# A graph-network kernel in groups: two entries in the first and last group, four between, and first products from features that TensorE turns

## The chip, the cores and the metric

The kernel runs on one core of a Trainium2 chip. The metric is the device time of one execution in microseconds (us), as the median of several runs. The engines are TensorE (PE: matrix products and transposes), VectorE (DVE), ScalarE (ACT), GpSimd (POOL, which here issues the indirect DMAs) and SyncE (SP, which issues plain DMAs). Each engine works through its own instructions in order.

## The reference

There are 32 batch entries of 512 nodes with 256 features, and one 512x512 matrix `adj` in which few cells are not zero. Four layers follow each other: a graph layer with a gate for each edge, two plain layers, and a second graph layer with other weights.

```python
def gnn(h, A, W1, b1, W2, b2, Wa, ba, Wm, bm, beta1, beta2, beta3):   # layers 0 and 3
    pre_u = einsum('bud,dk->buk', h, W1[:d])
    pre_v = einsum('bvd,dk->bvk', h, W1[d:])
    hidden = relu(pre_u[:, :, None, :] + pre_v[:, None, :, :] + b1)
    S = sigmoid(einsum('buvk,ko->buvo', hidden, W2)[..., 0] + b2[0])
    a_t = einsum('buv,bud->bvd', S * A, h)
    m_t = einsum('uv,bud->bvd', A, h) * h
    return beta1*h + beta2*(a_t @ Wa + ba) + beta3*(m_t @ Wm + bm)

def layer1(z):                                    # z + relu(A z W^T + b)
    return z + relu(einsum('bid,ed->bie', einsum('ij,bjd->bid', A, z), W) + b)

def layer2(x):
    feats = einsum('bni,oi->bno', x, W1)
    f1 = einsum('bno,o->bn', feats, W2) + b2[0]
    coefs = softmax(leaky_relu(f1[:, :, None] + f1[:, None, :]) + A, axis=-1)
    return einsum('bij,bjo->bio', coefs, feats) + bias2 + x
```

S is needed only where `adj` is not zero. The kernel computes it there alone.

## The kernel before, in words

**Groups.** The entries are worked on in eight groups of four (`NB = 4`). A group goes through five stages, each a Python generator whose pieces are woven into one program.

- `first` (line 806): for each entry, load the features h, turn them on TensorE (`turned`, line 571), and form the products with W1 (`pre`, line 582: lines 592 and 594 on TensorE, 596 to 600 on DVE and ACT). The products go to a table in DRAM, one row for each node and side, with the group's four entries beside each other (4 x 256 values, 4 KB). The turned features are written to DRAM as `xT` (line 819).
- `edges` (line 650) of layer 0, here called an edge round: 36 items of 128 edges. For an item POOL fetches 128 table rows with an indirect DMA (`fetch`, line 644), DVE adds the row of the other node (line 731) and takes relu times W2, and the sum over features comes either from DVE itself, one entry at a time (line 747), or from ACT (line 717) after one DVE instruction for all entries (line 739). After the sigmoid (lines 614, 618, 619) and the factor from `adj` (line 675), POOL puts 128 cells of four values into a DRAM array with another indirect DMA (`put`, line 637). The rows of the other node ("mine") come by plain loads from SP (line 692) or, for four items, by an indirect DMA.
- `middle` (line 839): loads the group's cells as dense matrices (`load`, line 766, 1 MB each, four of them), and then does for each entry the rest of layer 0, layers 1 and 2, and the first products of layer 3 (`middle_one`, line 876). ACT first copies one entry's matrix out of the four (`flat`, line 857); line 891 is its first product.
- `edges` of layer 3, with its own table and cells.
- `last` (line 1094): the rest of layer 3 for each entry: the products hWa and mhT, then the sums with S (line 1061) and with Wm (line 1073).

**The two ends.** For the first group the products hWa and mhT are made ahead of its middle (`middle_before`, line 824), from h (line 867) and from the turned features loaded back from `xT` (line 871, in `fresh`). Its middle then takes them as `given`. For the last group `last` is split: `last_before` (line 1016) makes all that doesn't need S, `last_behind` (line 1039) the sums with S. In the edge rounds of these two ends ACT does all of the sums and more buffers hold fetched rows (`spare`).

**The cells.** One pair of cell arrays for each layer is zeroed once (`zeros`, line 555, eight plain DMAs issued by POOL; layer 0 in the opening, layer 3 in `zeros_behind`, line 550, after a DVE memset), and each group writes the same cells again. A put waits for the zeros and for the loads of the group before.

**The order.** `weave` (line 454) sorts the pieces of all stages by due times that are written out by hand in `sparse_path` (line 1162): one group's middle is one unit long, the middle of group 0 starts at 0. `edge_times` and `spread` (lines 1130 to 1143) spread the pieces of a stage evenly. `first` and `last` fill in where a middle leaves room on TensorE. Due times set an order and nothing else; what is late then holds up what stands behind it on its engine.

```python
        start, end = (max(0.0, k - 0.47) for k in (t, t + 1))
        ...
        edges3 = edge_times(end + 0.003, end + 0.05, end + 0.48, end + 0.54)
        behind = end + 0.56, end + 1.16
```

Of the kernel before, what the change touches and what calls it, by code (L numbers as in the profile page):

```python
# [38 lines left out]
GROUP = NB * D  # L39
# [364 lines left out]
class Group:  # L404
# [3 lines left out]
    def __init__(self, sp, w, name):  # L408
        self.w = w
        self.table = sp.dram.tile([2 * N, GROUP], F32, name=f"table_{name}")  # L410
        self.cells = sp.cells[name[0]]
        self.layer = name[0]
        self.puts = [f"puts_{name}_{q}" for q in range(2)]
        self.written = [[], []]
        self.s = sp.grp.tile([P, ITEMS, NB], F32, name=f"s{name[0]}")
        self.self_s = sp.grp.tile([P, NC, NB], F32, name=f"self_s{name[0]}")
# [6 lines left out]
class Sparse:  # L423
# [3 lines left out]
    def __init__(self, ctx, m, counts, xr, outr, B):  # L427
# [7 lines left out]
            k: [self.dram.tile([CELLS + SPARE, NB], F32, name=f"cells_{k}{q}") for q in range(2)] for k in "03"  # L435
# [11 lines left out]
        self.later, self.bigs, self.given, self.marks = None, 0, None, {}  # L447
        self.main = None
        self.before = {(k, q): [] for k in "03" for q in range(2)}
# [80 lines left out]
    def setup(self):  # L530
# [4 lines left out]
        self.zero = self.act.tile([P, GROUP], F32, name="zero", tag="hWa3")  # L535
# [8 lines left out]
        self.zeros("0")  # L544
# [5 lines left out]
    def zeros_behind(self):  # L550
        self.behind(self.nc.vector.memset(self.zero, 0.0))
        self.zeros("3")
        yield

    def zeros(self, layer):
        for h, c in enumerate(self.cells[layer]):
            flat = c[0:CELLS, :].rearrange("(q p a) b -> q p (a b)", q=4, p=P)
            for q in range(4):
                ins = self.nc.gpsimd.dma_start(flat[q], self.zero)
                self.before[layer, h].append(ins.ins.name)  # L560
# [21 lines left out]
    def pre(self, g, b, hT):  # L582

        nc, w = self.nc, g.w
        rows = g.table.rearrange("(c p k) (b d) -> p c k b d", p=P, k=2, b=NB)
# [41 lines left out]
    def written(self, g, half, ins):  # L627

        ins = ins.ins
        self.tc.declare_no_dep(ins, group=g.puts[half], reason="no two of a group's puts share a cell")
        self.tc.add_to_no_dep_group(g.puts[half], ins)
        self.after(ins, self.before[g.layer, half], "cells zeroed, and read by the group before")
        g.written[half].append(ins.name)
# [14 lines left out]
    def edges(self, g, spare=(), own_tags=()):  # L650
# [12 lines left out]
        def own_1():  # L663
            self.sigmoid_of(own)
            diag = self.counts.diag.unsqueeze(2).to_broadcast([P, NC, NB])
# [6 lines left out]
        def run_1(ks):  # L672
            self.sigmoid_of(g.s[:, ks, :].rearrange(flat))
            value = e.value[:, ks].unsqueeze(2).to_broadcast([P, ks.stop - ks.start, NB])
# [7 lines left out]
        def fetch(n):  # L682
            if n == EARLY:
                for j, tag in zip(panels, own_tags):
                    mine[-j] = self.act.tile([P, GROUP], F32, name="mine_more", tag=tag)
# [3 lines left out]
            if c not in mine:  # L689
                t = self.gath.tile([P, GROUP], F32, name="mine", bufs=3)  # L690
# [7 lines left out]
            if tag := tags[n % len(tags)]:  # L698
                rows = self.act.tile([P, GROUP], F32, name="rows_more", tag=tag)
            else:  # L700
                rows = self.gath.tile([P, GROUP], F32, name="rows")
# [11 lines left out]
        def sums(k, rows):  # L713

            for b in range(NB):
# [11 lines left out]
        for k in range(ITEMS):  # L727
# [8 lines left out]
            if spare or k % 2 == 1 and k < ITEMS - 3:  # L736
                by_entry = rows.rearrange("p (b d) -> p b d", b=NB)
                w2 = w["W2bc"].unsqueeze(1).to_broadcast([P, NB, D])
# [4 lines left out]
            else:  # L743
                for b in range(NB):
# [21 lines left out]
    def load(self, g, layer):  # L766

        tiles, loads = [], [[], []]
        for c in range(NC):
            t = self.act.tile([P, N, NB], F32, name=f"SA{layer}", bufs=NC)  # L770
# [7 lines left out]
        for q, names in enumerate(loads):  # L778
            self.before[g.layer, q] = names
# [26 lines left out]
    def first(self, g, i):  # L806
# [8 lines left out]
        for b in range(NB):  # L815
            ahead = load(b + 1) if b < NB - 1 else None
# [7 lines left out]
    def middle_before(self, g0, i):  # L824

        self.given = []
        for b in range(NB):
            h, hT = self.fresh(i + b)
            hT = hT()
# [7 lines left out]
            self.given.append((hWa, mhT))  # L837

    def middle(self, g0, g3, i):
# [3 lines left out]
        given, self.given = self.given, None  # L843
        h, hT = self.fresh(i, given)
        hT = hT()
        hWa = None
        if not given:
# [3 lines left out]
        for b in range(NB):  # L851
# [24 lines left out]
    def middle_one(self, g0, g3, b, i, SA, keep, given):  # L876
# [3 lines left out]
        if given:  # L880
            hWa, mhT = given[b]
# [19 lines left out]
        more = b < NB - 1  # L901
        if more:
            keep[0], turned = self.fresh(i + 1, given)
# [24 lines left out]
        if more:  # L928
            keep[1] = turned()
            ahead = None if given else self.hWa(g0, keep[1], 0)  # L930
# [85 lines left out]
    def last_before(self, g, i):  # L1016

        self.ends = []
        for b in range(NB):
# [19 lines left out]
    def last_behind(self, g, i):  # L1039
        SA = self.load(g, 3)  # L1040
        for b in range(NB):
# [52 lines left out]
    def last(self, g, i):  # L1094
# [6 lines left out]
        for b in range(NB):  # L1101
            for hWa in self.hWa(g, hT, 3):
                yield
            if done is not None:
                nc.sync.dma_start(self.outr[i + b - 1], done)
                if b < NB - 1:
# [3 lines left out]
            if b < NB - 1:  # L1110
# [3 lines left out]
        nc.sync.dma_start(self.outr[i + NB - 1], done)  # L1114
# [11 lines left out]
FIRST, LAST, AHEAD = even(NB * 5 + 1), even(NB * 8 + 1), even(NB * 4 + 1)  # L1126
ENDS, BEHIND = even(NB * 6 + 1), even(NB * 2 + 1)
# [18 lines left out]
def middle_shares(given):  # L1146


    hWa = [] if given else [1.7, 1.7]
    shares = list(hWa)  # L1150
    for b in range(NB):
        more = hWa if b < NB - 1 else []
        shares += [] if given else [2.8, 2.8]
# [8 lines left out]
def sparse_path(ctx, m, counts, xr, outr, B):  # L1162
# [3 lines left out]
    last = B // NB - 1  # L1166
# [4 lines left out]
        (sp.zeros_behind(), spread(even(2), 0.15, 0.2), ""),  # L1171
    ]
    for t in range(last + 1):
        g0, g3 = Group(sp, m.g0, f"0_{t}"), Group(sp, m.g3, f"3_{t}")
        start, end = (max(0.0, k - 0.47) for k in (t, t + 1))

        if t == 0:
            first = spread(FIRST, -0.385, -0.30)
            edges0 = edge_times(-0.292, -0.27, -0.03, -0.02, LEAD_AT_ENDS)
        elif t == 1:  # L1180
            first = spread(FIRST, -0.28, -0.06)
# [268 lines left out]
```

## Time and profile before

| what | value |
|---|---|
| runs of the kernel before | 2991.82, 2996.85, 2997.82 us; median 2996.85 us |
| profiled execution | 2998.45 us, with a span of 2996.8 us |
| PE busy | 2690.0 us (90%) |
| DVE busy | 2307.1 us (77%) |
| POOL busy | 1555.3 us (52%) |
| ACT busy | 1336.8 us (45%) |
| moved by DMA | 677.30 MB, mean 226 GB/s |
| POOL fetches of rows (line 646) | 552 of 1230 ns |
| POOL puts of cells (line 639) | 576 of 1211 ns |

The span is what the profiler sees of one execution; the profiled execution's own time lies 1.65 us above it. A line such as L731 is line 731 of the kernel before. "Busy" counts an engine's own instructions, not its waits; a share is one of the whole span and hides that stages differ. The page also cuts the span into 40 equal slices and gives each engine's busy tenths in each. "PEclk" is the clock that TensorE was granted, in tenths of full speed. A row in a table of windows gives the window, its length, and the busy time (with the number of instructions) of PE, of PE's weight loads, of DVE, ACT and POOL, then the granted clock, the share of the DMA engines and the bytes moved. In a timeline, the bracket at the end of a row gives the idle time before it and what ended that.

### The profile page before, as it was taken

The numbers are of one execution on the slowest core, as the hardware profiler recorded it, in microseconds if no ns is written. First come the engines' busy times: TensorE is split into PE (matmuls) and PEld (weight loads), VectorE is DVE, ScalarE is ACT, GpSimd is POOL, SyncE is SP. The second block draws the span as 40 slices with busy tenths as digits, with TensorE's granted clock in tenths as the row PEclk, the third lists the DMA queues.
The fourth block names the chain that finished last, engine by engine and source line by source line (L and its number), as shares of the span: only waits on it lengthen the run. The fifth ranks groups of instructions, "written<-read, shape, count | busy, mean of one in ns | idle before, by whom it ended". The sixth has DMA issues, their size and how long they took to land. (4 is left out here: it accounts for less than half of the span.)

```text
span 2996.8 us, 32453 instructions
## 1 busy us (share of the span) xinstructions
PE 2690.0 (90%) x8645; PEld 1613.9 (54%) x8646; DVE 2307.1 (77%) x6035; ACT 1336.8 (45%) x4101; POOL 1555.3 (52%) x1328
## 2 busy tenths in 40 slices
PE   6367787989998999989999899989999899988998
PEld 3134344545664566546664466646565466644666
DVE  6874786889588885988778885888858896783494
ACT  3553454445344443544344443445434453453262
POOL 2662463646445673556536464466735564361183
PEclk9678998999999999999999999999999999999999
DMA  8875657796678867787677866687677866663474
GB/s 268 286 225 169 213 174 221 233 300 203 217 217 269 268 211 227 230 262 254 209 222 247 275 207 230 216 268 253 211 228 236 303 227 197 208 211 102 148 244 150
DMA packets 302143, 677.30 MB, mean 226 GB/s; under 512 B 52608, under 2 KB 170880, under 8 KB 293760
## 3 DMA queue, kind: packets, MB, share of 16 engines
q0 software_dynamic: 122688, 414.40, 42.9%
q1 hardware_dynamic: 160304, 223.52, 23.0%
q10 hardware_dynamic: 18960, 37.24, 3.4%
q8 instruction: 70, 1.15, 0.2%
q14 instruction: 121, 0.99, 0.1%
HBM read 529.02 MB, written 146.01 MB: 225 GB/s over the span
## 5 line engine op out<-in xcount | busy, mean ns | idle before, releaser
L646 POOL DMA_INDIRECT rows<-table,iv x552 | 679.0, 1230 | 795.5 <-DMA table<-puv 262.7
L639 POOL DMA_INDIRECT cells<-s,cell x576 | 697.6, 1211 | 420.6 <-DVE s L675 243.2
L731 DVE TENSOR_TENSOR rows<-rows,mine 128x1024 f32<-128x1024 f32 x552 | 666.4, 1215 | 101.4 <-DMA rows<-table,iv 72.8
L717 ACT ACTIVATE rows<-rows 128x256 f32<-128x256 f32 x1088 | 439.6, 406 | 445.4 <-DVE rows L739 396.6
L46 PE MATMUL pst<-adj,h 128*128 128x512 f32 x1024 | 452.2, 592 | 0.0
L747 DVE SCALAR_TENSOR_TENSOR rows<-rows,L_gnn_W2bc 128x256 f32<-128x256 f32 x1120 | 414.0, 417 | 1.6
L739 DVE SCALAR_TENSOR_TENSOR rows<-rows,L_gnn_W2bc 128x1024 f32<-128x1024 f32 x272 | 329.4, 1213 | 0.4
L46 PEld LDWEIGHTS pst<-adj,h 128*128 128x128 f32 x1024 | 192.8, 190 | 219.9 <-issue 217.6
L46 PE MATMUL pst<-L_gnn_Wa,hT 128*128 128x256 f32 x1024 | 248.8, 393 | 62.9 <-DMA hT<-xT 57.8
L46 PEld LDWEIGHTS pst<-L_gnn_Wa,hT 128*128 128x128 f32 x1024 | 198.9, 199 | 103.0 <-issue 59.2
L46 PE MATMUL pst<-eT,feats 128*128 128x512 f32 x512 | 237.7, 619 | 10.9 <-ACT eT L1004 10.9
L46 PE MATMUL pst<-adjT,zW 128*128 128x512 f32 x512 | 228.2, 599 | 11.6 <-ACT zW L916 9.7
L596 DVE TENSOR_TENSOR puv<-pst,bc_L_gnn_b 128x256 f32<-128x256 f32 x256 | 104.9, 416 | 162.4 <-DMA table<-puv 89.2
L597 ACT COPY puv<-pst 128x256 f32<-128x256 f32 x256 | 93.2, 371 | 288.1 <-DVE puv L596 225.9
L1061 PE MATMUL pst<-hWa,SA 128*128 128x256 f32 x896 | 220.3, 400 | 0.0
L1061 PEld LDWEIGHTS pst<-hWa,SA 128*128 128x128 f32 x896 | 213.8, 328 | 3.7 <-issue 1.7
L717 ACT ACTIVATION_READ_ACCUMULATOR rows<-rows 128x1 f32 x1088 | 204.7, 188 | 0.0
L860 ACT COPY flat<-SA 128x512 f32<-128x512 f32 x128 | 136.7, 1128 | 136.6 <-issue 62.9
L891 PE MATMUL pst<-flat,hWa 128*128 128x512 f32 x448 | 196.8, 592 | 0.0
L592 PE MATMUL pst<-w_L_gnn_W,hT 128*128 128x512 f32 x256 | 141.5, 681 | 53.9 <-ACT hT L579 36.5
L46 PEld LDWEIGHTS pst<-eT,feats 128*128 128x128 f32 x512 | 99.9, 198 | 133.2 <-issue 113.3
L46 PEld LDWEIGHTS pst<-adjT,zW 128*128 128x128 f32 x512 | 96.5, 191 | 133.4 <-issue 114.0
(176 smaller groups left out, 3984.2 us busy)
## 6 DMA issues: line engine op xcount, KB each, us to landing
table<-puv SPq DMA_DIRECT2D x256, 256.0 KB
SA<-cells POOLq DMA_DIRECT2D x64, 1024.0 KB
h<-in_x_dram SPq DMA_DIRECT2D x64, 512.0 KB
mine<-table SPq DMA_DIRECT2D x64, 512.0 KB
hT<-xT SPq DMA_DIRECT2D x36, 512.0 KB
xT<-hT ACTq DMA_DIRECT2D x32, 512.0 KB
x2T<-yT SPq DMA_DIRECT2D x32, 512.0 KB
x2s<-x ACTq DMA_DIRECT2D x64, 256.0 KB
```

Of the source, the lines that this page charges most:

```text
L46: nc.tensor.matmul(out, lhsT, rhs, start=(n == 0), stop=(n == len(pairs) - 1))
L592: nc.tensor.matmul(pp, hT[:, 0, ks], w["W1"][:, 0::DC, :], start=True, stop=False)
L596: nc.vector.tensor_tensor(puv[:, 0, :], pp[:, 0:D], w["b1bc"], ALU.add)
L639: ins = self.nc.gpsimd.indirect_dma_start(out=g.cells[half], out_offset=bass.IndirectOffsetOnAxis(ap=at, axis=0), in_=s, in_offset=None)
L646: self.nc.gpsimd.indirect_dma_start(out=rows, out_offset=None, in_=g.table, in_offset=bass.IndirectOffsetOnAxis(ap=at, axis=0))
L717: self.behind(nc.scalar.activation(part, part, AF.Identity, accum_out=g.s[:, k, b : b + 1]))
L731: self.behind(nc.vector.tensor_tensor(rows, rows, other, ALU.add))
L739: nc.vector.scalar_tensor_tensor(by_entry, by_entry, 0.0, w2, ALU.max, ALU.mult)
L747: nc.vector.scalar_tensor_tensor(part, part, 0.0, w["W2bc"], ALU.max, ALU.mult, accum_out=at)
L860: self.nc.scalar.copy(flat[:, r, :], SA[r][:, :, b])
L891: nc.tensor.matmul(pz, hWa[:, r, cs], flat[:, r, :], start=(r == 0), stop=False)
L1061: self.nc.tensor.matmul(pz[:, k * D : (k + 1) * D], SA[r][:, cs, b], hWa[:, r, :], start=(r + k == 0), stop=(alone and k == 1 and r == NC ...
```

## The change

The 32 entries go in nine groups of 2, 4, 4, 4, 4, 4, 4, 4 and 2. A group carries its size `n`, and tables, cells, row buffers and loops go by it. There are cell arrays for both sizes, each zeroed: those for layer 0 with two entries in the opening, those with four entries a little later, and layer 3's two sizes in the first middles. `middle_before` still makes four entries' hWa and mhT: the two of group 0 and the first two of group 1. It turns their features on TensorE with `turned` in place of loading `xT`; the middle still loads `xT` for its own use. The due times are written anew. Cut to its core:

```diff
-GROUP = NB * D
+FEW = 2
 class Group:
-    def __init__(self, sp, w, name):
+    def __init__(self, sp, w, name, n):
-        self.table = sp.dram.tile([2 * N, GROUP], F32, name=f"table_{name}")
+        self.table = sp.dram.tile([2 * N, n * D], F32, name=f"table_{name}")
-        self.cells = sp.cells[name[0]]
+        self.cells = sp.cells[name[0], n]
 ...
-    def zeros_behind(self):
-        self.behind(self.nc.vector.memset(self.zero, 0.0))
-        self.zeros("3")
-        yield
+    def zeros_behind(self, of):
+        for k in of:
+            self.behind(self.nc.vector.memset(self.zero, 0.0))
+            self.zeros(*k)
+            yield
 ...
     def middle_before(self, g0, i):
-        self.given = []
         for b in range(NB):
-            h, hT = self.fresh(i + b)
-            hT = hT()
+            h, _ = self.fresh(i + b)
+            hT = self.turned(h, "hT1")
 ...
-            self.given.append((hWa, mhT))
+            self.given[i + b] = hWa, mhT
 ...
+LENGTHS = {0: 0.4, 1: 0.87}
+GIVEN = {0: FEW, 1: NB - FEW}
 ...
-    last = B // NB - 1
+    sizes = [FEW] + [NB] * ((B - 2 * FEW) // NB) + [FEW]
+    last = len(sizes) - 1
 ...
-        (sp.zeros_behind(), spread(even(2), 0.15, 0.2), ""),
+        (sp.zeros_behind([("0", NB)]), spread(even(2), -0.2, -0.15), ""),
+        (sp.zeros_behind([("3", FEW), ("3", NB)]), spread(even(3), 0.15, 0.45), ""),
 ...
-    for t in range(last + 1):
-        start, end = (max(0.0, k - 0.47) for k in (t, t + 1))
+    at, end = 0, 0.0
+    for t, n in enumerate(sizes):
+        start, end = end, end + (0.4 if t == last else LENGTHS.get(t, 1.0))
         if t == 0:
-            first = spread(FIRST, -0.385, -0.30)
+            first = -0.385, -0.345
             edges0 = edge_times(-0.292, -0.27, -0.03, -0.02, LEAD_AT_ENDS)
+            edges3 = edge_times(end + 0.003, end + 0.02, end + 0.3, end + 0.33)
+            behind = end + 0.4, end + 0.8
         elif t == 1:
-            edges0 = edge_times(0.02, 0.07, start - 0.06, start - 0.04)
+            edges0 = edge_times(0.01, 0.03, start - 0.05, start - 0.03)
 ...
         if t == last - 1:
-            edges3 = edge_times(end + 0.003, end + 0.05, end + 0.46, end + 0.5)
-            behind = end + 0.7, end + 1.06
+            edges3 = edge_times(end + 0.003, end + 0.04, end + 0.38, end + 0.4)
+            behind = end + 0.44, end + 0.6
         if t == last:
-            end -= 0.2
-            edges3 = edge_times(end + 0.003, end + 0.02, end + 0.45, end + 0.46, LEAD_AT_ENDS)
-            behind = end + 0.29, end + 0.45
+            edges3 = edge_times(end + 0.003, end + 0.02, end + 0.3, end + 0.31, LEAD_AT_ENDS)
+            behind = end + 0.21, end + 0.3
 ...
-            streams.append((sp.last_behind(g3, t * NB), spread(BEHIND, end + 0.5, end + 0.6), ""))
+            times = spread(even(BEHIND * n + 1), end + 0.35, end + 0.42)
+            streams.append((sp.last_behind(g3, at), times, ""))
```

In `middle_one`, an entry's hWa and mhT are looked up by its number (`if i in given`), so that a middle may have some entries' products given and make the others'.

## The prediction

> **What bounds the kernel now.** I read the busy shares by slice first. TensorE (PE) is at nine tenths nearly everywhere except in the first ten or so slices, and there its granted clock falls too.
>
> ```profile
> PE   6367787989998999989999899989999899988998
> DVE  6874786889588885988778885888858896783494
> PEclk9678998999999999999999999999999999999999
> ```
>
> Then I cut the span where the first matmul of line 891 of each group's middle stands, and where the last of line 594 ends, and asked for busy times by window (columns: window, length, busy us of PE, weight loads, DVE, ACT, POOL, granted clock, DMA share, GB/s). I call the stretches opening, main 0, main 1, a steady main (mains 2 to 6 last 344.6, 346.1, 349.4, 343.6 and 343.6), main 7 and tail.
>
> ```profile
> 0.00:245.20 245.20, 135.81 (x389) 74.36 (x391) 174.92 (x437) 114.28 (x426) 127.88 (x125) 0.80 0.79 260
> 245.20:485.20 240.00, 195.90 (x561) 103.66 (x560) 159.06 (x423) 113.08 (x291) 94.74 (x87) 0.89 0.56 183
> 485.20:824.20 339.00, 308.86 (x985) 181.41 (x984) 277.24 (x757) 154.20 (x462) 193.00 (x162) 0.97 0.74 237
> 1168.80:1514.90 346.10, 328.44 (x1073) 197.35 (x1072) 281.93 (x764) 155.01 (x464) 188.71 (x161) 0.99 0.73 238
> 2551.50:2817.60 266.10, 246.51 (x779) 145.37 (x778) 165.22 (x432) 107.73 (x285) 87.89 (x79) 0.97 0.47 149
> 2817.60:2996.80 179.20, 160.16 (x576) 121.87 (x574) 121.03 (x166) 72.60 (x317) 99.96 (x80) 0.96 0.66 218
> ```
>
> The reader is to see that a steady main is PE-bound (328 of 346 us), while opening and main 0 hold 109 and 44 us of idle PE. The tail holds only 19. So an earlier first main is what there is to win, and the price is paid where a main becomes short against the edge round beside it.
>
> Third, the opening and the round that follows it, and entries of main 7 (its last has no round items beside it):
>
> ```profile
> 82.00:235.00 153.00, 70.49 (x185) 38.93 (x184) 121.73 (x244) 79.86 (x341) 101.97 (x80) 0.71 0.76 253
> 240.00:451.00 211.00, 170.33 (x485) 89.38 (x483) 147.51 (x388) 100.56 (x267) 93.61 (x85) 0.90 0.57 184
> ...
> 2551.50:2626.80 75.30, 74.57 (x253) 46.87 (x252) 59.16 (x148) 33.94 (x99) 30.32 (x27) 1.00 0.66 213
> 2626.80:2695.60 68.80, 57.96 (x165) 31.71 (x164) 59.50 (x150) 36.00 (x113) 47.34 (x41) 0.90 0.65 203
> 2757.60:2817.60 60.00, 60.00 (x199) 37.06 (x198) 18.15 (x42) 14.76 (x30) 0.00 (x0) 1.00 0.08 27
> ```
>
> The first two edge rounds run from 82 to 235 and from 240 to 451. The same cut for the adds of line 731 alone (one to an item) says that main 7's first two entries have 16 and 18 items beside them:
>
> ```profile
> 2551.50:2626.80 75.30, 18.67 (x16) 1.00 0.66 213
> 2626.80:2695.60 68.80, 21.25 (x18) 0.90 0.65 203
> ```
>
> Last, waits in the opening and the end of the chain:
>
> ```profile
> PE pst L46 <- DMA hT<-xT: 57.8, 4, 25.7
> ```
>
> ```profile
> 220.70 1.24 POOL L639 DMA_INDIRECT cells<-s,cell  x1 [7.47 <-ACT big L791]
> ```
>
> ```profile
> 2958.43 5.13 DMA SA<-cells
> 2963.60 27.92 PE pst L1061 x118
> ```
>
> **The change, part by part.** The order of both programs gives the counts. PE gains 32 instructions (4 entries x 8 transposes); POOL gains 168: two rounds of 76 (36 fetches, 4 panel or "mine" fetches, 36 puts), 8 cell loads, 8 zero writes. SP goes from 592 to 600: four hT loads go, two rounds bring 8 "mine" loads and 4 diagonal writes. No entry's work goes. PE work of an entry, by the chain's rows: middle 6.87 (L891) + 3.43 (L898) + 3.45 (L912) + 6.9 (yT) + 3.5 (L934) + 2.2 (turns) + 6.9 (feats) + 6.87 (first products) + 0.88 = 41.0; hWa and mhT 10.3; its `first` 0.87 + 6.87 = 7.7; its `last` 3.45 + 6.87 + 7.7 (L1061) + 3.45 = 21.5.
>
> *Opening, 245 to 198.* The first fetch starts at 81.9, when four entries are in the table. Entry two's table writes are issued at 52.4 for 3.5 us, and the first index list is ready at 57.2 (DVE, L394): with two entries the first fetch is at 57. Round 0 on DVE now takes 36 x (1.2 + 1.2) = 86 us and DVE is full (20 of 20 us) from 120 to 180; with rows of 512 in place of 1024 elements it is 43, so POOL takes over. POOL has 80 indirect DMAs here; before they took 1.27 us each (101.97 / 80) and 0.30 us of issue between two. With DVE eased I take 1.2 + 0.30: 80 x 1.5 = 120. The zeros for the four-entry cells now stand in the middle of this queue: 8 issues, 4.3 us (4.26 for 8 at 315 us). They add no wait if their DVE memset is early. With 6 us for the first items, the last put ends at 57 + 120 + 4 + 6 = 187. From the last put (234.1) to the first matmul of main 0 (245.2) are 11 now; I keep them, though the cell load is half as large: 198. Bounds: 1.24 per DMA (the shortest, 0.94 + 0.30) gives 178, and today's 1.57 with some 25 us of stalls, as now, gives 223.
>
> *Turned features by PE.* 32 transposes at 1.04 us for eight cost PE 4.2 us and 8 copies of 0.59 us cost ACT 4.7, both in an opening where PE is idle. What goes is the wait of 57.8 us for hT, behind which ACT held its copies, and POOL 7.5 us of puts. But the plain load of h is issued beside it, so most of the wait may stay:
>
> ```profile
> 199.50 0.37 SPq L867 DMA_DIRECT2D h<-in_x_dram  x1
> 200.22 0.34 SPq L871 DMA_DIRECT2D hT<-xT  x1
> ```
>
> If h lands as late as hT did, the gain is nothing, and the transposes and copies come on top: 0 to +9 us; if not, up to -15. I take 0. The trace has eight such transposes in 1.04 us at a granted clock of 0.66 to 0.78. The Trainium skill, "TensorE: Matmul & The Clock Gate", Part 4: PE-mode transpose, speaks against it: some 275 ns for one 128x128 transpose in a kernel, which do not count as activity that lifts the clock. By the page the 32 would cost 8.8 us in place of 4.2, an estimate that changes the sum by under 5 us.
>
> *Main 0, 240 to 146.* Two entries, 82 us of PE, and nothing else to fill PE with: `first` of the next group comes later. Beside them all of round 1: 36 adds x 1.14, 16 products x 1.14, 20 x 4 x 0.35 = 87 us of DVE, and 2 x 18.15 for the entries: 123, so 61.5 per entry. The row for that is main 7's second entry: 18 items, 59.5 us of DVE and 41 POOL instructions in 68.8 us. Scaled 71 per entry, 142, and 4 for the cell load behind the last put. POOL needs 75 x 1.5 + 12 zero issues (6.4) = 119: it fits. At the DVE share of 240 to 451 us (147.5 / 211 = 0.70) the same round takes 123 / 0.70 = 176.
>
> *Main 1, 339 to 301.* PE: 4 x 41 + 3 x 10.3 (two entries are given) + 4 x 7.7 + 2 x 21.5 = 269. Main 1 now has 298 by the same rows and takes 339, 41 more. With the second-layer round of two-entry rows (DVE about 45 us less) I take 32 idle; bounds 20 and 45.
>
> *Main 2: 339*, as main 1 now: the program holds the same PE work (298) and edge rounds there. *Mains 3 to 6: 4 x 345.4*, the mean of today's five steady ones.
>
> *Main 7: 328.* PE 4 x 41 + 4 x 10.3 + 2 x 7.7 + 4 x 21.5 = 307, and 21 idle (steady: 346 - 322 = 24).
>
> *Main 8, new: 142.* Two entries with PE 82 + 10 + 23 (a quarter of `last` of group 6) = 115 and the four-entry round 36 items: 123 of DVE. Main 7's first two entries now carry 34 items and 132 us of PE in 144.1 us. Less PE, more DVE: 142; bounds 130 and 176.
>
> *Tail, 179 to 151.* 7.3 from the last product to the first fetch, the round, 9.2 for the load, 27.9 for the sums, 5.3 for the output. The round takes 129.5 now with 13 POOL DMAs per 20 us (1.54) once DVE is full. Halved on DVE, POOL remains: 80 x 1.45 = 116; the load 8, the sums half, 14: 7.3 + 116 + 8 + 14 + 5.3 = 151; bounds 134 and 163. PE has 129 there (86 of `last`, 43 of the final group), 14 of it in the sums: covered.
>
> **Sum:** 198 + 146 + 301 + 339 + 1381.6 + 328 + 142 + 151 = 2987 against a span of 2996.8. That execution took 2998.45, 1.65 over its span, and the median shown is 2996.85; the two offsets cancel, so I forecast **2987 us**.
>
> A rule against the change: the Trainium skill, "Perfetto Trace Analysis", DMA Optimizations, holds that larger transfers use memory better and that 2 KB pieces gain by becoming 4 KB. Rows of two entries go the other way, 4 KB to 2 KB. The trace has 386 GB/s at a DMA share of 1.03 from 80 to 100 us with 4 KB rows, none with 2 KB. If by the page a 2 KB row cost as much as a 4 KB one, the opening would keep its DMA share of 0.76, and the sum would not move, since POOL sets it.
>
> **Rivals.** *Short mains don't cover a round (slower).* Round 1 has only two entries to hide behind, and nothing is queued on PE when they are done. At the DVE share of 0.70 main 0 takes 176 (+30), and main 8, likewise late, pushes POOL's last round back by some 12: 3029. It decides from a DVE share of about 0.79 down, where main 0 takes 156. For it: today's round 1 took 211 us, and POOL idles for ACT and DVE there; against it: 59.5 us of DVE in 68.8. *POOL at its shortest (faster still).* At 1.24 us per DMA opening (178) and tail (134) fall to 312 together in place of 349, and the h loads stall less (-5): 2945. For it: DMAs of 0.94 to 1.0 wherever DVE is quiet; against: 1.27 on average. *Nothing gained.* The steady mains take up no slack, so if the extra boundary costs 10 us more (the idle PE at 950 to 1000 is 8.7) the end is 2997; likewise if the opening still waits for its h loads as it did for hT, which would be the change not doing what it says.
>
> **How the numbers follow.** Forecast 0.45 (its own range 2965 to 3006: faster 0.31, same 0.09, slower 0.05), slower rival 0.30, faster rival 0.17, nothing 0.08. A measurement tells 0.2% from no change, 6 us. Faster 0.31 + 0.17 = 0.48, same 0.17, slower 0.35. The range leaves out a tenth at each end of these cases: 2945 to 3032.
>
> **What would show it.** First fetch near 57 and not 82; first line-891 matmul near 198; main 1 some 146 later; DVE share in main 0 over 0.8; POOL the busiest from 100 to 185 and in the tail; tail near 151. The forecast is wrong if main 0 or main 8 passes 160, or if PE waits for h in the opening for as long as it did for hT.

## The result, and the profile after

The changed kernel takes 3117.44 us (median of four runs, 3098.85 to 3128.23), the kernel before 2997.34 beside it: 1.0396 times as long, 95% interval 1.0351 to 1.0440. The forecast was 2987 us, and its range ended at 3032. On another chip, where the kernel before takes 2974.51 us, the ratio is 1.0300 (1.0279 to 1.0322). So the sign stands, and about a quarter of the size changes with the chip; the last section comes back to that.

The profiled execution took 3119.39 us with a span of 3117.7. In slices, each now of 77.9 us, PE has its low digits in the first seven (before: in the first ten of 74.9 us, on the whole less low) and again in the last three:

```profile
PE   5565587998989999999899998999899988999678
DVE  7738575877888598868888688958888686658652
PEclk8787798999999999999999999999999999999788
```

(A line such as L893 is now line 893 of the changed kernel.) Cut at the first line-893 matmul of each group (line 891 before) and at the last of line 597 (594 before), the stretches are opening, main 0, main 1, main 2, then (not shown) mains 3 to 6 with 343.5, 342.2, 349.8 and 347.1, main 7, the new main 8, and the tail. The columns are window, length, busy us of PE, weight loads, DVE, ACT and POOL, granted clock, DMA share, GB/s:

```profile
0.00:217.90 217.90, 121.52 (x373) 68.98 (x375) 132.51 (x415) 85.53 (x281) 115.86 (x130) 0.80 0.71 227
217.90:373.20 155.30, 96.13 (x266) 50.04 (x264) 119.64 (x317) 63.40 (x207) 90.78 (x84) 0.80 0.65 202
373.20:722.10 348.90, 295.47 (x881) 165.23 (x882) 236.15 (x680) 145.17 (x402) 179.07 (x164) 0.91 0.64 200
722.10:1061.00 338.90, 309.88 (x985) 181.36 (x984) 277.39 (x757) 154.63 (x462) 191.32 (x162) 0.97 0.74 237
2443.60:2780.00 336.40, 312.96 (x1026) 190.95 (x1025) 233.93 (x652) 136.38 (x388) 177.97 (x160) 0.97 0.63 191
2780.00:2929.60 149.60, 125.45 (x379) 73.11 (x378) 126.59 (x338) 62.74 (x207) 92.56 (x75) 0.89 0.64 197
2929.60:3117.70 188.10, 144.97 (x488) 103.50 (x486) 76.97 (x155) 42.28 (x171) 83.02 (x82) 0.87 0.44 135
```

The reader is to see main 1 and the tail: 53 and 43 us of idle PE, and a clock of 0.91 and 0.87 where the kernel before had 0.97 and 0.96. Set against the terms of the sum:

| stage | forecast | measured | miss |
|---|---|---|---|
| opening | 198 | 217.9 | +20 |
| main 0 | 146 | 155.3 | +9 |
| main 1 | 301 | 348.9 | +48 |
| main 2 | 339 | 338.9 | 0 |
| mains 3 to 6 | 1381.6 | 1382.6 | +1 |
| main 7 | 328 | 336.4 | +8 |
| main 8 | 142 | 149.6 | +8 |
| tail | 151 | 188.1 | +37 |

Against the kernel before, the same entry is the fair mark. The first entry starts 27 us earlier (217.9 for 245.2), the third 8 us later (373.2 for 365.5), the seventh 71 us later (722.1 for 651.2), and the 31st 84 us later (2780.0 for 2695.6); the end is 121 us later. So 98 us are lost between the first and the seventh entry, 13 in the 24 entries between, and 37 after the 31st.

In the opening, PE's longest wait has changed its name, not gone. It was for hT (57.8 us); it is for h now:

```profile
PE pst L581 <- DMA h<-in_x_dram: 41.4, 3, 24.1
```

The columns are total, times and longest. A fourth wait, of 18.3 us, stands before the same transposes, and the profile names nothing that ended it. In `early_end` below, whose opening is the same program, all four waits are for h:

```profile
PE pst L581 <- DMA h<-in_x_dram: 63.1, 4, 26.2
```

So PE waits for h in the opening for about as long as it did for hT. And the end of the chain of waits is no longer load, sums, output:

```profile
3069.95 10.33 PE pst L46 x32
...
3084.77 10.56 PE pst L46 x32
3095.33 3.64 PE pst L1075 x16
3098.97 13.83 PE pst L1063 x64
```

The round's last put was at 3056.8. Behind it PE still makes hWa and mhT of the last two entries (the rows of 10.33 and 10.56) before the last sums with the cells (L1063, the row of 13.83). The load of the cells did not wait for the round alone either; what let it go was PE, with the sums of group 7:

```profile
3065.40 2.22 POOL L775 DMA_DIRECT2D SA<-cells  x4 [7.65 <-PE pst L1063]
```

### The profile page after: what moved, and what is told of

Same layout as the page of the kernel before. It is cut to its first block, busy times and chain, and to the rows that moved or that the text cites. A ratio compares the mean times of both kernels' runs of the same rounds, so it can differ in the third digit from the quotient of the medians.

```text
span 3117.7 us, 33003 instructions
## 1 busy us (share of the span) xinstructions
PE 2722.6 (87%) x8677; PEld 1626.0 (52%) x8678; DVE 2330.5 (75%) x6369; ACT 1310.9 (42%) x3973; POOL 1700.0 (55%) x1496
## 4 chain that ended last, share of the span: by engine, by line
PE 41%; DVE 21%; DMA 12%; issue 7%; ACT 4%; POOL 2%; another core or an unknown queue 1%; SPq 0%; DVEq 0%; ACTq 0%; POOLq 0%
PE pst L46 20%; DVE rows L734 6%; DMA rows<-table,iv 6%; DMA table<-puv 5%; PE pst L1063 5%; DVE rows L750 4%; DVE rows L742 3%; PE pst L893 2%; PE pst L1075 2%; PE pst L595 2%; PE pst L597 2%; PE pst L914 2%; PE pst L936 2%; PE pst L900 1%; ACT flat L862 1%
## 5 line engine op out<-in xcount | busy, mean ns | idle before, releaser
L649 POOL DMA_INDIRECT rows<-table,iv x624 | 742.9, 1191 | 729.3 <-DMA table<-puv 200.8
L642 POOL DMA_INDIRECT cells<-s,cell x648 | 771.1, 1190 | 495.5 <-DVE s L678 303.4
L734 DVE TENSOR_TENSOR rows<-rows,mine 128x1024 f32<-128x1024 f32 (+1 forms) x624 | 689.8, 1113 | 172.6 <-DMA rows<-table,iv 139.8
L720 ACT ACTIVATE rows<-rows 128x256 f32<-128x256 f32 x1056 | 427.2, 407 | 473.2 <-DVE rows L742 429.8
L750 DVE SCALAR_TENSOR_TENSOR rows<-rows,L_gnn_W2bc 128x256 f32<-128x256 f32 x1200 | 445.6, 417 | 1.8
L742 DVE SCALAR_TENSOR_TENSOR rows<-rows,L_gnn_W2bc 128x1024 f32<-128x1024 f32 (+1 forms) x304 | 325.6, 1073 | 0.3
L1063 PE MATMUL pst<-hWa,SA 128*128 128x256 f32 x960 | 241.0, 406 | 15.6 <-ACT hWa L794 13.4
L1063 PEld LDWEIGHTS pst<-hWa,SA 128*128 128x128 f32 x960 | 229.0, 319 | 26.3 <-ACT hWa L794 16.1
L893 PE MATMUL pst<-flat,hWa 128*128 128x512 f32 x448 | 196.8, 592 | 0.0
L862 ACT COPY flat<-SA 128x512 f32<-128x512 f32 x128 | 129.7, 1071 | 141.7 <-issue 59.7
L1005 PE MATMUL pst<-ident,ex 128*128 128x128 f32 x512 | 87.1, 306 | 114.2 <-DVE ex L966 86.5
```

Source lines behind the costliest of these rows:

```text
L642: ins = self.nc.gpsimd.indirect_dma_start(out=g.cells[half], out_offset=bass.IndirectOffsetOnAxis(ap=at, axis=0), in_=s, in_offset=None)
L649: self.nc.gpsimd.indirect_dma_start(out=rows, out_offset=None, in_=g.table, in_offset=bass.IndirectOffsetOnAxis(ap=at, axis=0))
L720: self.behind(nc.scalar.activation(part, part, AF.Identity, accum_out=g.s[:, k, b : b + 1]))
L734: self.behind(nc.vector.tensor_tensor(rows, rows, other, ALU.add))
L742: nc.vector.scalar_tensor_tensor(by_entry, by_entry, 0.0, w2, ALU.max, ALU.mult)
L750: nc.vector.scalar_tensor_tensor(part, part, 0.0, w["W2bc"], ALU.max, ALU.mult, accum_out=at)
```

## The theories

**Order:** the loss is where pieces stand in the in-order program (the first products of entries 3 and 4 at the end of the opening, the sums at the end), and moving them takes it away. **Turning:** the turned features cost it. **Crowding:** the given entries of mains 0 and 1 are short on PE, and what paces them is the items of the edge rounds between their steps on DVE and ACT; the kernel before had one round beside four of them; now they have that round, the two-entry round of layer 3, and the four entries of `first` of group 2. Then moving PE work about does nothing. **Chain:** a given entry takes 80 us by its own steps. For the tail: **PE's sums** of group 7 set it, or **the round** does.

The runs fell on four chips: A (the kernel before took 2996.57 us there, medians), B (2983.49), C (2974.51) and D (2999.93, one execution). On which chip the two kernels above were profiled is not known. `no_round`, `tail_bare`, `tail_items` and the four runs on D are single executions. Stages are compared on one chip wherever the text says so; between `loaded` and `early_end`, whose main 1 is the same program on the same chip, main 1 differs by 9 us (342.0 and 351.1), so a few us in one stage tell nothing.

## Experiments on the opening and the turned features

**`loaded`**, chip A. In `middle_before`:

```diff
-            h, _ = self.fresh(i + b)
-            hT = self.turned(h, "hT1")
+            h, hT = self.fresh(i + b)
+            hT = hT()
```

> The changed kernel, but the four given entries load their turned features from memory, as the kernel before did (32 transposes and 8 copies fewer, four loads more). Order theory: what closes the opening is the chain of four given entries in PE's order, each of which waits for its loads on SP's queue; a load of hT comes on that queue in any case behind the load of h, so the opening stays within 10 us of 218 us and the time at 3117 +- 15. Turning theory (the turned features are what costs): the opening falls from 218 to about 200 us and the time to about 3097.

Measured: 3129.34 us, ratio 1.0436 (1.0372 to 1.0500); opening 235.1, PE's wait for hT 75.2 us in four times. `early_end` below has the changed kernel's opening, 222.3 on this chip. So in the opening the turned features save 13 us, where the one theory said under 10 and the other said a cost. The turning theory falls, and the forecast's 0 for this part was too little. When main 2 starts, 5 of the 13 us are left (726.9 for 731.5), and the totals (3124.84 in `early_end`) can't be told apart.

**`turned_alone`**, chip A: the same edit, the other way round, in the kernel before.

```diff
-            h, hT = self.fresh(i + b)
-            hT = hT()
+            h, _ = self.fresh(i + b)
+            hT = self.turned(h, "hT1")
```

> The kernel before, eight groups of four, with only the turned features of the given entries made by TensorE. Order theory: in the kernel before the round on DVE and POOL closes the opening (last put at 234 us, first product of the middle at 245), the chain of given entries is hidden beside it, and taking away the 58 us wait for hT gives at most the 7.5 us of puts that it held: 2985 to 3000 us. Turning theory: transposes and copies cost 5 to 20 us in the opening, 3002 to 3017.

Measured: 2993.02 us, ratio 0.9987 (0.9968 to 1.0007); opening 238.9, for 245.2 in the profile of the kernel before, which is another execution. The order theory had given it at most 7.5 us; in the total it can't be told from nothing.

**`two_given`**, chip A:

```diff
-        for b in range(NB):
+        for b in range(FEW):
...
-GIVEN = {0: FEW, 1: NB - FEW}
+GIVEN = {0: FEW}
...
-            streams.append((sp.middle_before(g0, 0), spread(even(AHEAD * NB + 1), -0.15, -0.03), ""))
+            streams.append((sp.middle_before(g0, 0), spread(even(AHEAD * FEW + 1), -0.15, -0.03), ""))
```

> The changed kernel, but only the two entries of group 0 have their first products made in the opening; the two others of the first four make them in main 1. Order theory: the opening closes with the load of the cells (SA at 182.7 us, copies at 196) and falls from 218 to 200 +- 5 us; main 1 takes up its 21 us of products inside its 54 us of idle PE and stays at 349 +- 8: 3097 to 3105 in all. Rival, rounds that cost (main 1 is long because its rounds hold PE): opening 200, but main 1 grows by the 21 us, 3117 +- 8.

Measured: 3117.51 us, ratio 1.0410 (1.0375 to 1.0445); opening 196.9, main 0 164.9, main 1 354.6. The opening falls as foretold, and PE now waits for what the round delivers, the copies of the cells:

```profile
PE pst L893 <- ACT flat L862: 33.4, 1, 33.4
```

So in the changed kernel it was the products of entries 3 and 4, with the loads of h that they wait for, standing in front of main 0 in PE's order, that closed the opening. But main 0 takes back 11 of the 25 us and main 1 4 (`early_end`, same chip: 222.3, 153.5, 351.1), and the total can't be told from that of `early_end` (3124.84). The order theory is right on the opening and wrong on what it is worth; the rival had the total, but saw the growth in main 1.

## Experiments on mains 0 and 1

**`no_round`**, chip B. The generator of the round yields its pieces and does nothing, for layer 3 of group 0:

```diff
+        if skip:
+            for _ in range(LEAD + ITEMS + TAIL):
+                yield
+            return
```

> The changed kernel without the whole edge round of the second layer of group 0 (its fetches, adds, products, sums, puts and the diagonal write), the one that stands beside the first two entries of main 1; the two entries' last stage reads the zeros of the cells. PE's program is the same. Crowding theory (the given entries are short on PE, and what stretches them is the items that stand between their steps on DVE and ACT): the two entries fall from 185 to 120-140 us together, main 1 from 349 to about 300, and the time to about 3070. Rival, chain theory (a given entry with nothing to fill PE takes 80 to 90 us by its own steps): they stay within 10 us of 185 us, main 1 above 335.

**`no_round1`**, chip D: the same for layer 0 of group 1.

> The changed kernel without the edge round of group 1 (four entries, 36 items) that stands beside the two entries of main 0; main 1 then reads the zeros of the cells. Crowding theory, as the round left out in main 1 showed it: main 0 falls from 154 to 110 to 125 us (82 of PE). Rival, chain theory (an entry with only its own 41 us of PE needs some 70 us for its steps): main 0 stays above 140.

Measured, the first two entries of main 1 with the round (`tail_bare` below, which has this start unchanged, on the same chip) and without:

```profile
367.80:538.10 170.30, 138.82 (x393) 71.25 (x394) 113.93 (x354) 73.23 (x199) 93.56 (x91) 0.93 0.71 221
```

```profile
373.80:516.80 143.00, 129.87 (x392) 68.93 (x393) 64.51 (x184) 56.74 (x120) 9.41 (x12) 0.96 0.51 171
```

and main 0 with its round (`again2`, the changed kernel once more, on the same chip) and without:

```profile
221.90:379.00 157.10, 97.05 (x265) 50.51 (x263) 119.54 (x317) 63.34 (x207) 91.19 (x85) 0.79 0.64 202
```

```profile
214.80:317.00 102.20, 89.24 (x265) 48.77 (x264) 33.13 (x83) 37.96 (x72) 8.50 (x16) 0.92 0.42 154
```

The matmuls are the same (the counts in the first bracket, to one), and the time falls by 27 and by 55 us. Without its round main 0 takes 51 us an entry, less than either theory had said. Main 1 as a whole falls from 332.7 to 304.8 on chip B, to within 4 us of the forecast. None of the rows has an engine at its limit: DVE is busy for 0.67 and 0.76 of the time with the rounds. In main 0 of the changed kernel the long waits are PE's for DVE, ACT's for DVE and POOL's for ACT:

```profile
PE pst L1005 <- DVE ex L966: 36.4, 7, 15.5
...
ACT rows L720 <- DVE rows L742: 28.0, 10, 5.4
POOL rows L649 <- ACT rows L720: 26.3, 5, 21.1
```

So the entries are lengthened by the round, and it looks like waiting in turn. Which engine's share of the round does it is not shown: the runs take its work from DVE, ACT, POOL and the DMA queues at once, and PE's clock rises with it (0.79 to 0.92 in main 0). `no_round` was foretold 120 to 140 us for the two entries and came to 143, just outside and far from the chain theory's 185 +- 10.

**`first_earlier`**, chip B:

```diff
-            first = start - 0.82, start - 0.56
+            first = (0.02, 0.3) if t == 2 else (start - 0.82, start - 0.56)
```

> The changed kernel with the first stage of group 2 (its 31 us of PE) due in main 0 (0.02 to 0.3 of the unit) in place of the first half of main 1 (0.45 to 0.71). Nothing is added or left out. Crowding theory (DVE and ACT, not PE, pace the four given entries): main 0 grows by as much as main 1 loses, the first group of the four starts main 2 within 12 us of 1061, time 3105 to 3130. Rival, order theory (PE's idle 59 us in main 0 is only unfilled): main 0 grows by under 10, main 1 loses 25 to 35, and the round of the four-entry group starts at about 515 instead of 532: 3085 to 3098.

Measured: 3075.40 us, ratio 1.0331 (1.0300 to 1.0362), on a chip on which the kernel before is faster too (2983.49), so that the foretold times don't serve and the stages must. Main 0 is 171.2 (152.3 in `tail_bare` on this chip), main 1 313.8 (332.7): 19 us go from the one to the other, and none is left over. That is crowding: main 0 has 59 us of idle PE, but no room.

**`turned_first`**, chip C: the same in the kernel before, with the turned features.

```diff
-            first = spread(FIRST, start - 0.82, start - 0.56)
+            first = spread(FIRST, *((0.1, 0.46) if t == 2 else (start - 0.82, start - 0.56)))
```

> The kernel before (eight groups of four) with the turned features made by TensorE and the first stage of group 2 due at 0.1 to 0.46 of the unit, in main 0, in place of 0.71 to 0.97, in main 1. Filling theory (main 0 of the kernel before has 44 us of idle PE, and only work put there earlier can use it): main 0 grows from 240 to 250-255, main 1 falls from 339 to 312-320, time 2975 to 2985 against 2997. Rival, crowding (the items of round 1 on DVE and ACT pace main 0, so each matmul put there delays an entry): main 0 grows by the 25 us or more that main 1 loses, 2990 to 3005.

Measured: 2972.75 us, ratio 0.9999 (0.9986 to 1.0012). Main 0 grows from the 240 of the kernel before (234.6 in `turned_alone`; neither profile is from chip C) to 267.1, main 1 falls from 339 (344.3) to 313.6. Together they last 580.7 us, for 579.0 and 578.9. Crowding again, in groups of four.

**`two_first`**, chip B: the edits of `two_given` and `first_earlier` together.

> As the run before, and in addition only the two entries of group 0 have their first products made in the opening. Crowding theory: the opening falls to about 197 us as in the kernel with two given entries alone, and mains 0 and 1 give it back: 3105 to 3125. Order theory: 197 for the opening, main 0 at 170, main 1 at 335, together 20 to 30 us earlier: 3085 to 3097.

Measured: 3052.83 us, ratio 1.0242 (1.0211 to 1.0272); opening 188.6, main 0 184.2, main 1 303.4. Together the two edits keep what the opening gains: main 2 starts at 676.2, in `tail_bare` at 700.5. Alone the one kept 11 us (chip A) and the other 3. With both, the round of group 2 puts its first cells at 524 us, with `first_earlier` alone or neither on this chip at 550 and 551, so main 1 can end earlier by what main 0 got. These 20 to 30 us the order theory had foretold; crowding alone doesn't give them. Whether the two edits help one another or only add up, no run shows: 24 and 14 us lie little farther apart than two executions do.

## Experiments on the tail

**`early_end`**, chip A:

```diff
-            behind = end + 0.44, end + 0.6
+            behind = end + 0.402, end + 0.52
...
-            behind = end + 0.21, end + 0.3
+            behind = end + 0.12, end + 0.2
```

> The changed kernel with other due times at the end only: the final sums of group 7 at 0.402 to 0.52 of the unit in place of 0.44 to 0.6, the products before the last round's sums at 0.12 to 0.2 after the last main in place of 0.21 to 0.3. Order theory: PE's 129 us of work are then done beside the round, whose last put stays at about 127 us after the last main (3057 now); after it come the load (8), the sums (14) and the output (5), so the tail falls from 188 to 155 +- 8 us and the time to 3077 to 3092. Rival, round cost (DVE and ACT, which the sums need, hold the round back when the sums come earlier): the round ends 20 to 30 us later, the tail stays at 180 to 190, 3110 to 3120.

Measured: 3124.84 us, ratio 1.0420 (1.0381 to 1.0458), tail 187.0, last put 127 us after the last main. The round is not held back, and PE trails all the same. Both theories fail here. A stretch of slow matmuls lies in this tail too (last section), so the run doesn't tell what the due times are worth without it; `end_combo` below does.

**`tail_bare`**, chip B, and **`tail_items`**, chip C, leave out work of the last round:

```diff
-            self.behind(nc.vector.tensor_tensor(rows, rows, other, ALU.add))
+            if not bare:
+                self.behind(nc.vector.tensor_tensor(rows, rows, other, ALU.add))
...
-            if spare or k % 2 == 1 and k < ITEMS - 3:
+            if bare:
+                pass
+            elif spare or k % 2 == 1 and k < ITEMS - 3:
...
-            nc.vector.tensor_tensor(g.s[:, ks, :], g.s[:, ks, :], value, ALU.mult)
+            if bare:
+                nc.vector.memset(g.s[:, ks, :], 0.5)
```

> The changed kernel without the work of the last round on DVE and ACT (adds, products, sums, sigmoid; the values put are a constant): its fetches, puts, loads of mine and PE's program are the same. Theory of the tail (PE's sums of group 7 trail because the copies and adds that they need stand in ACT's and DVE's queues between items that come at POOL's pace): PE is through before the round's last put, the round ends 100 to 116 us after the last main, and the tail falls from 188 to 130-150 us. Rival (PE's slow matmuls, one in 1.4 to 2.8 us from 3027 to 3049 with nothing that releases them, set the tail): the stretch is there again and the tail stays above 165.

Measured: tail 140.9, but main 8 173.6. Puts of a constant wait for no fetch, so the round's 36 puts moved ahead into main 8, and the run doesn't tell what it was made for. `tail_items` mends that:

```diff
+            if bare:
+                by_entry = rows.rearrange("p (b d) -> p b d", b=g.n)
+                self.behind(nc.vector.tensor_scalar(g.s[:, k, :], by_entry[:, :, 0], 1.0, None, ALU.mult))
```

> The changed kernel, in whose last round the products and sums of the 36 items are left out (a two-column copy of the added row stands in their place, so that each put still waits for its fetch and add). POOL's program and PE's are the same. Theory of the tail (PE's work trails because its copies on ACT and adds on DVE stand behind items that wait for POOL's fetches): the items still come at POOL's pace, so PE still trails by most of it, the round ends at about 120 after the last main and the tail is 165 to 180. Rival (the time of the items on DVE and ACT makes PE trail): PE is through before the last put, tail 140 to 155.

Measured: tail 185.2, last put 118.0 us after the last main (174.6 and 120.9 in `again` on this chip). Without the products and sums the last put comes 3 us earlier and the tail is not shorter; the 10 us more are not explained. By this one run, the time of the items on DVE and ACT is not what makes PE trail.

**`again2`**, **`half_sums`** and **`no_sums`**, chip D: the changed kernel, and the same with two or none of group 7's four entries made in `last`:

```diff
+            if b >= few:
...
+                for _ in range(LAST):
+                    yield
+                done, h = h, ahead
+                continue
```

> The changed kernel, as the measure for the three others on this chip. Without the stretch of slow matmuls its stages are those of the run before (opening 211, main 0 154, main 1 333, main 8 148, tail 175); with it the tail is 187 to 191.

> The changed kernel, in which the last stage of group 7 makes two of its four entries; the two others are written out as they were loaded (43 us of PE left out, all of it in the tail; the round is the same). Theory that PE's work behind the short last main sets the tail: it falls by 18 to 25, to about 152 to 157. Rival (the round, the load and the final sums set it, whatever PE has beside them): it falls by under 8.

> The same with none of the four entries made (86 us of PE left out). Theory that PE's work sets the tail: once PE is through before the last put, more makes no difference: the round, load, sums and output alone, 148 to 153 us, at most 6 less than with two entries. Rival (the round itself is held back by the sums in DVE's and ACT's queues): the last put comes 10 us or more earlier after the last main (121 now) and the tail falls below 142.

The tails, in this order:

```profile
2927.90:3116.40 188.50, 146.37 (x489) 104.69 (x487) 76.92 (x155) 42.33 (x172) 83.30 (x82) 0.86 0.45 138
```

```profile
2924.30:3079.90 155.60, 105.13 (x328) 72.89 (x326) 68.65 (x143) 39.65 (x167) 83.78 (x82) 0.80 0.53 157
```

```profile
2924.60:3080.20 155.60, 49.84 (x168) 35.20 (x166) 60.82 (x131) 37.57 (x164) 83.07 (x82) 0.66 0.44 130
```

With half of the sums the tail is 33 us shorter, and with none no shorter still, to the tenth; the theory that PE's work sets the tail holds, and the rival's "under 8" falls. In both runs the last put comes 125 to 126 us after the last main, in `again2` 128.5, so the round takes what it takes. This settles the tail: the round, its load, the final sums and the output are 155.6 us, and above that lies the work of group 7, PE's matmuls with the copies and adds between them.

**`again`** and **`end_combo`**, chip C. `end_combo` has the edits of `two_first` and of `early_end`.

> The changed kernel itself once more, for its spread and for the stretch of slow matmuls in the tail (13 of them in 23 us from 3027, nothing released them). Theory that the stretch belongs to the kernel: it is there again, the tail is 185 to 192 us and the ratio to before 1.036 to 1.044. Rival, the stretch belongs to the chip or the execution (three other kernels of this shape had none, with tails of 172 to 174): it is absent, the tail is 172 to 176 and the time about 14 us less, ratio about 1.034.

> The changed kernel with first of group 2 in main 0, two given entries, and the sums of the end due earlier (all three of the earlier runs' edits). If the parts add up: the start as in the run with the first two edits (main 2 begins 45 us earlier than in the changed kernel), and the tail as there, 174 or 3 to 10 less: ratio to before 1.020 to 1.025. If the earlier sums hold the round back: 1.026 to 1.03.

Measured: `again` 3060.06 us, ratio 1.0300 (1.0279 to 1.0322), with no slow stretch in the tail, 174.6 us, as the rival had it (the stretch goes with the chip or the execution); `end_combo` 3034.02, ratio 1.0207 (1.0190 to 1.0225), opening 186.6, main 0 185.0, main 1 303.2, tail 171.1. The parts add up: 23 us at the start (main 2 begins at 674.8, in `again` at 698.0), 3.5 in the tail. It is the best of the kernels with groups of two, and still 60 us behind the kernel before. So on this chip 26 of the 86 us lost lie in where the work was placed, and 60 do not.

## Why the prediction was wrong, step by step

- **What bounds the kernel:** right in that the steady mains hold no slack (main 2 and mains 3 to 6 to 1 us). The step from "opening and main 0 hold 109 and 44 us of idle PE" to "an earlier first main is what there is to win" failed: the first main did come 27 us earlier, and mains 0 and 1 and the tail lost more. The idle PE of main 0 could not be used: some 30 us of matmuls due there lengthened it by 19 to 32 (`first_earlier`, `turned_first`).
- **Opening, 198:** the round came as worked out (first fetch at 57.1 for 57, last put at 183.6 for 187), and with the round as the last to end the opening is 196.9 (`two_given`). The step that failed is that the round ends the opening: PE's own chain of four given entries, with its loads of h, ends after it. It cost 20. The rival "nothing gained" had named this wait for h.
- **Turned features, 0:** undervalued by 13 in the opening (`loaded`), inside the bounds of -15 to +9. The reason given, that h lands as late as hT did, came true (63.1 us of waiting for h in `early_end`, 57.8 for hT before); what it missed is that in the changed kernel hT would be waited for longer still, 75.2 us.
- **Main 0, 146:** the mechanism (round 1 paces two entries) is right: 157 with, 102 without it. DVE's work was priced well (119.6 us for 123), its share of the time too high (0.77 for 0.84), and the term was 9 too small.
- **Main 1, 301:** the term that was mis-sized most. "I take 32 idle; bounds 20 and 45" was read off a main of full entries. Measured are 53 us of idle, and 295 us busy for 269 of full-clock work. Of the 48 us, 28 are the second-layer round beside the given entries (chip B, 332.7 to 304.8); 16 are the step from the execution on chip B to this one, with single stalls of up to 8.3 us and the lower clock, and 4 are left. "With the second-layer round of two-entry rows (DVE about 45 us less)" was taken for a relief; it stood beside entries that bring 41 us of PE work of their own, and not the 51 of a full entry.
- **Main 7 and 8, 328 and 142:** 8 too small each, 5% for main 8 where main 0 has 6%. Not tested by a run.
- **Tail, 151:** the round and what follows it, 155.6, is right to 5. "PE has 129 there ...: covered" failed: it costs 33 on chip D and 19 on chip C (174.6 less 155.6, from two chips). Main 8 ends 4 us after the last put of the round of group 7 (2926.0 and 2929.6), so all 86 us of its sums fall into the tail. To be covered, PE had to do 115 of the 129 us, all but the last sums, before the load of the cells is issued, 136 us after the last main (3065.4); it was busy for 98 us of the 136, in part at half clock. The slow stretch (16.9 us of idle PE with no releaser), waits for ACT's copies of hWa (13.4) and a clock of 0.87 left it short. The kernel before had more PE in its tail (160 us busy), and its last put came 136 us after the last main. Rows of half the size brought that to 127, and the sums then stood out beyond it.
- **Rivals and signs:** the slower rival had the right sign, and its condition was met (DVE's share of main 0 is 0.77; it decides from 0.79 down). But its two places, main 0 and main 8, hold +9 and +8, not +30 and +12. The two places that made most of the loss, main 1 and the tail, were in no rival. Of the signs that were to show the forecast wrong, main 0 and main 8 stayed under 160; the wait for h came.

On the clock: the granted clock is at half for 370 us of the span, and for 245 before, and PE's busy time is 2722.6 us for 2690.0, 33 more, for matmuls that add 4.2. The Trainium skill, "TensorE: Matmul & The Clock Gate", Terms, puts the penalty at the throttled time times the missing share of the clock. By that the 125 us more would cost some 62, an estimate. The trace shows about half of it: PE is busy in 206 us of the half-clock time, in 142 before, and waits in the rest; half of the 64 us more is 32. The rule and the trace agree in kind: of the 125 us, 41 lie in main 1 and 33 in the tail, where PE has its idle gaps, and these are paid a second time in slower matmuls.

## What to carry to other kernels

Idle time of one engine is not room: before moving work into a gap, find out what paces the gap, for example by leaving out what stands beside it, and price a stage by a row that has the same work on *all* engines. Making the first and last group smaller shortens the parts in which nothing overlaps, but each group brings its whole edge round, and a short main can neither hide that round nor the sums that come behind it. When a sum calls work "covered", add it up against the window with the engine's usual share of idle, and ask where it goes if the cover ends.

## What the hardware showed that was not expected

In the changed kernel's tail PE issues single matmuls 1.4 to 2.8 us apart, in a stretch of 22 us, and nothing releases them (timeline; the bracket gives the idle time and its cause):

```profile
3037.96 0.58 PE L46 MATMUL pst<-L_gnn_Wa,hT 128*128 128x256 f32 x1 [0.83 <-issue]
3040.07 0.58 PE L46 MATMUL pst<-L_gnn_Wa,hT 128*128 128x256 f32 x1 [1.53 <-issue]
3042.86 0.58 PE L46 MATMUL pst<-L_gnn_Wa,hT 128*128 128x256 f32 x1 [2.20 <-issue]
3045.66 0.59 PE L46 MATMUL pst<-L_gnn_Wa,hT 128*128 128x256 f32 x1 [2.21 <-issue]
```

The distances come in steps of 0.7 us (2.1 and twice 2.8 in these rows), and the granted clock is at half for most of the stretch. Stretches like this, of 7 to 15 matmuls that start 1.2 to 3.0 us apart, lie in the tail of the changed kernel, `loaded`, `two_given`, `early_end`, `again2`, `half_sums` and `no_round1`; all but the first of these are known to be from chips A and D, and their tails are 187 to 192 us where all sums are made. In `half_sums` the stretch is there and the tail is 155.6 us: it costs only where PE's work sets the tail. On chips B and C (`no_round`, `first_earlier`, `two_first`, `again`, `end_combo`) there is none, and the tails are 171 to 175; `no_sums`, on D, has none either, and nor has `tail_items`, on C, whose tail of 185.2 is not explained. What makes them is open: no run was made that could tell it. The tails with and without differ by some 14 us, about a tenth of the loss, but not all of it need be the stretch: the last put too stands some 4 to 11 us later after the last main on A and D (125 to 129 us, for 117 to 121).
